# A graph layer with routed experts: tile 5 changes its group, the third group's slots go from 192 to 176, the last tile's steps stand one tick apart, and the third group's second biases are added by tile and share

## The chip, the cores and the metric

The kernel runs on one core of one Trainium2 chip. The metric is device time in microseconds (us) of one execution; less is better. The core has five engines that run beside each other and meet through semaphores: TensorE (PE: matmuls), VectorE (DVE), ScalarE (ACT), GpSimd (POOL, here it issues the gathers and scatters) and SyncE (SP, issues transfers). Loads of weights into the PE array are listed apart, as PEld.

## The reference, cut to what matters

There are 3125 nodes of 256 features and 100,000 edges, sorted by their target node (many more edges end at low nodes). The layer adds to the input an edge part (a maximum over the incoming edges of each node) and an attention-like part, and then a part in which a router picks two of eight experts for each node:

```python
xn = _layernorm(x)
x = x + gnn(xn, src, dst) + mix(xn)      # gnn: relu(theta(x_dst - x_src) + phi(x_src)),
                                         # maximum over the edges of each dst
# routed experts, on xt = layernorm(x)
probs = softmax(xt @ Wr + br)
top_p, top_idx = top_k(probs, 2)
weights = top_p / top_p.sum(-1)
xn = normalised(xt)
xe = xn * ln_g[e] + ln_b[e]              # for each expert e of 8
h  = gelu(xe @ W1[e] + b1[e])            # 256 -> 1024
y  = h @ W2[e] + b2[e]                   # 1024 -> 256
x  = x + sum of the two picked experts' y, times weights
```

All is computed in float32. `b2` is what is called the second bias.

## The kernel before, in words

**Tiles, groups, steps.** The nodes are 25 tiles of 128. The edges are walked from the highest target to the lowest. They are dealt out over 128 lanes (partitions), so one step handles 128 edges: one gather on POOL (line 107, `g<-b_d,srcI`) brings 128 rows of 256, and one fold on DVE (line 366) carries a running maximum along each lane. There are 755 such steps, in four groups. `GROUPS` says which tiles a group has, and `STEPS` how many steps its edges take: before, tiles 12 to 24 in 240 steps, tiles 6 to 11 in 161, tiles 1 to 5 in 228 and tile 0 in 126. Folded rows are stored to `s_d`, and a tile later fetches its nodes' rows from there with one gather each (`r<-s_d,end_i`).

**What follows a group.** When a group's last edge is folded, `carry` (lines 369 to 390) hands the maxima over from lane to lane: transposes on PE (L373), a scan on DVE (L378), transposes back (L384), a copy (L389). Then each tile of the group goes through `token_tile` (lines 422 to 495): selection matmuls (L445), a sum on DVE, moments, a scaling on ACT (`xt`, L471), transposes (L482), the router's matmul (L489, L491) and the top two (L494). For each half of the group's tiles `dispatch` works out weights (`shares`) and places (`slots`), and scatters the tiles' rows into the experts' lots in DRAM (`xs_d`, line 114). `CAPS` is the number of places an expert has in a group. The group then joins the queue of expert units (`Stream`): for each expert, eight steps f of `hp` (L615), gelu (L617) and, one unit later, `yp` (L639). A unit's `yp` matmuls are laid beside the next unit's `hp` matmuls; the last unit's close the stream alone. Before it is copied out, each `yp` gets the second bias of its expert from a matmul on 8 rows (L748). Results go to `ys_d` and are gathered again by `combine` (`g<-ys_d,from_i`), where L1299 weighs and adds them, and an `out` transfer on SP stores them.

**The last group.** Tile 0 alone is the fourth group. It isn't scattered: `dense_tile` runs all eight experts on its 128 rows and adds them with the router's weights (L822, L824). It starts when tile 0 is routed and the expert stream is through. Tile 0 needs two more things: the last six folded rows, picked by matmuls (L1278) with ones that `last_ends` prepares (lines 1245 to 1272), and the maxima of the first four nodes from edges beyond the 755 steps, which `first_maxima` (lines 1203 to 1240) works out on DVE from the whole of `b_d`, 100 operations in all. `dense_half` loads half of an expert's weights (1,024 KB) into a buffer that has come free. Combines wait for the flag `shared`, which stands for tile 0's weights being worked out; of the ten wide buffers' users at the end, several wait for an earlier user's `out` transfer.

**What sets the order.** PE, DVE, ACT and SP run in an order that a planner in the program writes out. Its unit is a tick, one gather issued on POOL (`TICK` stands for 1.25 us). Every piece of work is a generator that says by `yield n` after how many ticks its next step is to be placed. A queue of tasks with due times puts all pieces in one order, and a step placed later stands later in its engine's queue, ready or not. `on_pe` books time on PE, and the expert stream places its next step by it:

```python
def room(least=0.25):
    return max(least, clock["pe"] - clock["now"] - 2)
```

In `token_tile`, `at_once` shortens the distances between a tile's steps; before, to two ticks at most, for the third group and for tile 0.

Of the kernel before, what the change touches and what calls it, by code (L numbers as in the profile page):

```python
# [40 lines left out]
GROUPS = ((12, 25), (6, 12), (1, 6), (0, 1))  # L41
STEPS = (240, 161, 228, 126)
CAPS = (512, 256, 192)
LOT = (256, 256, 192)
# [23 lines left out]
def gps_layer(ctx: ExitStack, tc: tile.TileContext, x, src, dst, thetaT, phiT, gbias, wq, wkvT,  # L68
# [300 lines left out]
    def carry(pool, ps, g, last, chain, carried):  # L369
# [5 lines left out]
        yield 3  # L375
# [5 lines left out]
        yield 2  # L381
# [4 lines left out]
        yield 3  # L386
# [35 lines left out]
    def token_tile(work, ps, i, r1, slices, carried, top, top_i, newton=False, then=None,  # L422
                   also=None, at_once=False):
# [4 lines left out]
        def after(ticks):  # L428
            return min(ticks, 2) if at_once else ticks
# [67 lines left out]
    def shares(ro, i0, i1, top, top_i, made, wait=0):  # L497
# [9 lines left out]
        pick = ro.tile([P, 2, nt, E], F32, name="pick")  # L507
# [92 lines left out]
    class Units:  # L600
# [3 lines left out]
        def __init__(self, ps, act, whole=False):  # L604
            self.ps, self.act, self.behind, self.whole = ps, act, None, whole

        def run(self, e, w1t, xe, w2t, done, between, parts, part):
# [16 lines left out]
            self.behind = [hT, w2t, done, {}, parts, part]  # L624

        def second(self, f):
# [3 lines left out]
            hT, w2t, done, yp, per, part = self.behind  # L630
# [4 lines left out]
            for k in range(f * per, (f + 1) * per):  # L635
                r, q = k // FC, k % FC
                if q == 0:
                    yp[r] = self.ps.tile([P, D], F32, name="yp")
                nc.tensor.matmul(yp[r][0:part, :], hT[q][:, r * part:(r + 1) * part], w2t[:, q, :], start=(q == 0),  # L639
                                 stop=(q == FC - 1 and self.whole))  # L640
# [11 lines left out]
    class Stream:  # L652
# [29 lines left out]
        def rows(self, v):  # L682
            if 2 * v < len(self.lots) and ("xs", v) not in self.held:
                xs = self.held["xs", v] = self.at(v % 2)
                move(nc.scalar, self.as_two(xs, v), self.two(xs_d, v))
# [29 lines left out]
        def go(self):  # L715
# [5 lines left out]
            while True:  # L721
# [23 lines left out]
                def done(r, yp, u=u, ys=ys):  # L745
                    g, e, h = self.lots[u]
                    n = self.half(u)
                    nc.tensor.matmul(yp[0:n, :], ident[0:E, e:e + 1].to_broadcast([E, n]), b2_sb, start=False, stop=True)  # L748
# [17 lines left out]
                for _ in units.run(e, w1t, self.held["xe", u], w2t, done, between, 2, self.half(u)):  # L766
                    yield room()
# [13 lines left out]
    def dense_tile(act, ps, mm, i, shared, w, next_w, order=range(E), ready=None):  # L781
# [36 lines left out]
        units = Units(ps, act, True)  # L818
        for k, e in enumerate(order):
# [13 lines left out]
            for _ in units.run(e, w[e][0], held["xe", e], w[e][1], done, between, 1, P):  # L833
# [268 lines left out]

    def dispatch(g, half, i0, i1, top, top_i, taken):

        ro = at_hand["route"]
        while not all(i in routed for i in range(i0, i1)) or len(taken) < half:
# [4 lines left out]
        rest = shares(ro, i0, i1, top[:, at:at + i1 - i0, :], top_i[:, at:at + i1 - i0, :], made,  # L1111
                      15 if g == G - 2 and half == 0 else 0)
        start(rest, clock["now"] + next(rest))
        yield from slots(ro, mm, g, half, i0, i1, made[0], taken)
        yield 3 if g == G - 2 else 9
# [7 lines left out]
    def group(g):  # L1123
# [7 lines left out]
        start(carry(at_hand["tok"], mm, g, clock["last"], chain, carried), clock["now"] + (2 if g == G - 1 else 0))  # L1131
        yield STORED if g < G - 1 else 0
        if g == G - 1:
# [4 lines left out]
                              newton=True, then=lambda: start(dense), also=ends, at_once=True))  # L1138
# [413 lines left out]
```

## Time and profile before

| what | us |
|---|---|
| median of 3 runs | 1233.48 |
| the three runs | 1220.97, 1233.55, 1233.48 |
| the profiled execution's own time | 1227.71 |
| its span, first to last instruction | 1225.8 |
| PE busy in the span | 936.1 (76%) |
| POOL busy | 886.6 (72%) |
| DVE busy | 677.0 (55%) |
| ACT busy | 326.9 (27%) |
| mean granted PE clock | 0.857 |

The page's second part cuts the span into 40 slices of 30.6 us; a digit is the busy share of an engine in tenths. A row of its fifth part names line, engine, operation, result<-operands and count, then busy time and mean ns of one, then the idle time of the engine just ahead of it and what ended it. In a timeline the columns are start, duration, engine, line, operation and, in brackets, the idle time before and what released the instruction.

### The profile page before, as it was taken

The page shows a single profiled execution, that of the slowest core. Times are in us where ns is not written, and L with a number is a line of the kernel's source. Part 1 is how long each engine was busy: PE and PEld are TensorE (multiplying, and loading weights), DVE is VectorE, ACT ScalarE, POOL GpSimd, SP SyncE. Part 2 cuts the span into 40 slices and gives each one's busy share as a digit, 9 for nine tenths or more (in the row PEclk, how much of TensorE's full clock was granted, in tenths as well). Part 3 has the DMA queues.
Part 4 walks back from the last instruction along what each step waited for, and adds up shares of the span by engine and source line. Part 5 has one row for each costly group of instructions (what it writes and reads, how often), then busy time and mean ns, then how long its engine had stood idle before and what let it go on. Part 6 is the DMA issues. An engine that isn't in the chain of part 4 may idle for free.

```text
span 1225.8 us, 13367 instructions
## 1 busy us (share of the span) xinstructions
PE 936.1 (76%) x3931; PEld 671.4 (55%) x3931; DVE 677.0 (55%) x1989; ACT 326.9 (27%) x763; POOL 886.6 (72%) x911
## 2 busy tenths in 40 slices
PE   6547766736923449599999999999994619999895
PEld 4324333323301334268888788888883408786794
DVE  7669766675336682333338845564565843333533
ACT  4212222210101232043333333333330204332241
POOL 6677777777777777777767777777777777776433
PEclk9778988876965557889999999999996559999898
DMA  8668877666686763468887888999997559996583
GB/s 280 210 206 284 296 243 240 224 226 206 214 287 200 256 222 138 158 236 288 300 278 239 292 279 310 326 317 368 398 373 278 191 185 331 394 385 206 164 341 89
DMA packets 104268, 320.52 MB, mean 261 GB/s; under 512 B 20982, under 2 KB 44399, under 8 KB 92666
## 3 DMA queue, kind: packets, MB, share of 16 engines
q0 software_dynamic: 44032, 119.73, 30.8%
q1 hardware_dynamic: 29740, 115.08, 23.9%
q10 hardware_dynamic: 30414, 84.76, 19.5%
q8 instruction: 33, 0.54, 0.2%
q14 instruction: 49, 0.40, 0.1%
HBM read 192.18 MB, written 127.31 MB: 261 GB/s over the span
## 4 chain that ended last, share of the span: by engine, by line
PE 39%; DMA 23%; POOL 16%; issue 10%; DVE 10%; ACT 1%; ACTq 0%; POOLq 0%; DVEq 0%; SPq 0%
DMA g<-b_d,srcI 18%; POOL g L107 15%; PE yp L639 15%; PE hp L615 14%; DVE g L366 4%; DMA g<-ys_d,from_i 3%; PE yp L748 3%; PE bp L241 2%; PE mm L403 2%; DMA r<-s_d,end_i 1%; PE mm L401 1%; PE trf L693 1%; POOL xs_d L114 1%; PE tr L234 1%; PE am L445 0%
## 5 line engine op out<-in xcount | busy, mean ns | idle before, releaser
L107 POOL DMA_INDIRECT g<-b_d,srcI x755 | 739.4, 979 | 237.3 <-issue 203.2
L366 DVE SCALAR_TENSOR_TENSOR g<-g,cut 128x256 f32<-128x256 f32 x751 | 363.2, 484 | 345.3 <-DMA g<-b_d,srcI 326.5
L639 PE MATMUL yp<-w,hT 128*128 128x256 f32 (+1 forms) x1120 | 295.4, 386 | 5.3 <-DVE o L824 5.3
L615 PE MATMUL hp<-xe,w 128*128 128x256 f32 (+2 forms) x1216 | 285.2, 361 | 4.5 <-issue 1.7
L615 PEld LDWEIGHTS hp<-xe,w 128*128 128x128 f32 x1216 | 217.2, 195 | 39.8 <-issue 11.9
L617 ACT ACTIVATE hT<-hp,sm 128x256 f32<-128x256 f32 (+2 forms) x320 | 141.2, 441 | 326.2 <-PE hp L615 325.3
L639 PEld LDWEIGHTS yp<-w,hT 128*128 128x128 f32 (+1 forms) x1120 | 202.1, 186 | 44.3 <-issue 11.5
L1007 PE MATMUL kv<-wkv,xn_lo 128*128 128x512 f32 x96 | 52.8, 701 | 42.0 <-DVE kn L1025 28.2
L1007 PE MATMUL kv<-wkv,xn_hi 128*128 128x512 f32 x104 | 59.1, 722 | 31.1 <-DVE kn L1025 31.1
L107 POOL DMA_INDIRECT g<-ys_d,from_i x48 | 45.8, 955 | 42.5 <-DVE g L1299 14.8
L445 PE MATMUL am<-cr,oh 128*128 128x257 f32 x88 | 38.9, 574 | 33.6 <-DVE r L450 26.3
L1222 DVE SCALAR_TENSOR_TENSOR xn_lo<-xn_lo,no_edge 128x256 f32<-128x256 f32 x96 | 46.1, 480 | 28.5 <-DMA xn_lo<-b_d 28.5
L1007 PEld LDWEIGHTS kv<-wkv,xn_lo 128*128 128x128 f32 x96 | 20.7, 226 | 66.2 <-issue 63.2
L1007 PEld LDWEIGHTS kv<-wkv,xn_hi 128*128 128x128 f32 x104 | 22.9, 232 | 58.6 <-issue 54.5
L445 PEld LDWEIGHTS am<-cr,oh 128*128 128x128 f32 x88 | 21.7, 277 | 42.6 <-issue 32.7
L401 PE MATMUL mm<-bias,ones 1*128 1x512 f32 x50 | 31.8, 719 | 16.8 <-ACT x_sb L408 13.5
L748 PE MATMUL yp<-b_sb,ident 8*128 8x256 f32 (+1 forms) x128 | 43.9, 422 | 0.0
L1011 ACT ACTIVATE sq<-kv 128x1024 f32<-128x1024 f32 x25 | 25.5, 1019 | 52.7 <-PE kv L1007 52.7
L1019 ACT ACTIVATE rsk<-var,eps 128x16 f32<-128x16 f32 x25 | 7.7, 307 | 118.1 <-DVE var L1016 118.1
L704 ACT ACTIVATE xe<-trf,sm 128x256 f32<-128x256 f32 (+1 forms) x64 | 31.6, 547 | 24.0 <-PE trf L693 24.0
L1030 PEld LDWEIGHTS dots_p<-kn,vn 128*128 128x128 f32 x200 | 26.7, 197 | 19.1 <-issue 17.5
L1030 PE MATMUL dots_p<-kn,vn 128*128 128x128 f32 x200 | 27.6, 282 | 9.0 <-DVE kn L1025 9.0
(285 smaller groups left out, 978.3 us busy)
## 6 DMA issues: line engine op xcount, KB each, us to landing
s_d<-g SPq DMA_DIRECT2D x80, 1024.0 KB
w<-in_w ACTq DMA_DIRECT2D x84, 512.0 KB
w<-in_w ACTq DMA_DIRECT2D x6, 2048.0 KB
g<-b_d,srcI POOLq DMA_INDIRECT x755, 4.4
s_d<-g SPq DMA_DIRECT2D x13, 896.0 KB
xn_hi<-xs_d ACTq DMA_DIRECT2D x12, 512.0 KB
xs_d<-zero ACTq DMA_DIRECT2D x8, 512.0 KB
b_d<-bt SPq DMA_DIRECT2D x5, 640.0 KB
```

The lines of the kernel that those rows point to most:

```text
L107: got = nc.gpsimd.indirect_dma_start(out=to, out_offset=None, in_=table, in_offset=row_index(index))
L366: nc.vector.scalar_tensor_tensor(g[:, j, :], last, cut[:, t:t + 1], g[:, j, :], op0=OP.add, op1=OP.max)
L401: nc.tensor.matmul(am, ones[0:1, :], bias, start=True, stop=False)
L445: nc.tensor.matmul(r2, picks[k], carried[g], start=(k == 0), stop=(k == len(slices) - 1))
L615: nc.tensor.matmul(hp[:, 0:n], w1t[:, c, f, :], xe[:, c, 0:n], start=(c == 0), stop=(c == 1))
L617: nc.scalar.activation(hT[f][:, 0:n], hp[:, 0:n], AF.Gelu, bias=sm[:, 4 + f, e:e + 1])
L639: nc.tensor.matmul(yp[r][0:part, :], hT[q][:, r * part:(r + 1) * part], w2t[:, q, :], start=(q == 0), stop=(q == FC - 1 and self.whole))
L704: nc.scalar.activation(xe[:, c, 0:n], self.held["tr", u][:, c, 0:n], AF.Identity, bias=sm[:, 2 + c, e:e + 1], scale=sm[:, c, e:e + 1])
L748: nc.tensor.matmul(yp[0:n, :], ident[0:E, e:e + 1].to_broadcast([E, n]), b2_sb, start=False, stop=True)
L1007: nc.tensor.matmul(kv[:, k, :], xnT(i, c), wkv[:, c, k * INNER:(k + 1) * INNER], start=(c == 0), stop=(c == 1))
L1030: nc.tensor.matmul(dots_p[:, r, :], vn[:, r * P:(r + 1) * P], knf[:, r * P:(r + 1) * P], start=(i == 0 and r == 0), stop=(i == NT - 1), sk ...
L1222: nc.vector.scalar_tensor_tensor(of_k[:, k, :], b, no_edge[:, k, i:i + 1], of_k[:, k, :], op0=OP.add, op1=OP.max)
```

## The change

It has six parts.

- Tile 5 goes from the third group to the second, with the steps of its edges: `GROUPS` and `STEPS`. The sum of the steps stays 755.
- The third group's places for an expert go from 192 to 176.
- The third group's second biases are no longer added to each expert's `yp` by L748. A new function, `second_biases`, adds them to the tiles' rows in `x_sb`, from the two weights and the picked experts, with a transpose and one matmul for each tile. `Units` gets `whole` with each unit, so that the accumulation ends with the last `yp` matmul where no bias follows. The `pick` tile that it reads gets a buffer of its own for the half whose weights come late.
- The last group's `carry` steps and tile 0's `token_tile` steps stand one tick apart; `carry` is placed half a tick after the last fold and not two. The third group's scatter is placed one tick after its slots and not three.
- The first transfer of the third group's rows to the experts is two transfers, one for each of its two experts.
- `first_maxima` pauses while the third group's tiles are routed. The load of expert 0's first half and `last_ends` follow at its end; before, they followed 40 ticks after the third group had joined the queue.

```diff
-GROUPS = ((12, 25), (6, 12), (1, 6), (0, 1))
-STEPS = (240, 161, 228, 126)
-CAPS = (512, 256, 192)
-LOT = (256, 256, 192)
+GROUPS = ((12, 25), (5, 12), (1, 5), (0, 1))
+STEPS = (240, 195, 194, 126)
+CAPS = (512, 256, 176)
+LOT = (256, 256, 176)
...
 def carry(pool, ps, g, last, chain, carried):
...
-        yield 3
+        yield 3 if g < G - 1 else 1
...
-        yield 2
+        yield 2 if g < G - 1 else 1
...
-        yield 3
+        yield 3 if g < G - 1 else 1
...
 def token_tile(...):
-            return min(ticks, 2) if at_once else ticks
+            return min(ticks, at_once) if at_once else ticks
...
 def shares(...):
-        pick = ro.tile([P, 2, nt, E], F32, name="pick")
+        pick = ro.tile([P, 2, nt, E], F32, name=f"pick{int(wait > 0)}")
...
 class Units:
-                                 stop=(q == FC - 1 and self.whole))
+                                 stop=(q == FC - 1 and whole))
...
 class Stream, rows:
-                move(nc.scalar, self.as_two(xs, v), self.two(xs_d, v))
+                to, of = self.as_two(xs, v), self.two(xs_d, v)
+                if self.lots[2 * v][0] == G - 2 and self.lots[2 * v][1] == 0:
+                    for k in range(2):
+                        move(nc.scalar, to[:, k], of[:, k])
+                else:
+                    move(nc.scalar, to, of)
...
 done:
-                    nc.tensor.matmul(yp[0:n, :], ident[0:E, e:e + 1].to_broadcast([E, n]), b2_sb, start=False, stop=True)
+                    if g < G - 2:
+                        nc.tensor.matmul(yp[0:n, :], ident[0:E, e:e + 1].to_broadcast([E, n]), b2_sb, start=False,
+                                         stop=True)
...
+    def second_biases(i0, i1, pick):
+        ro = at_hand["route"]
+        for t in range(i1 - i0):
+            i = i0 + t
+            by = ro.tile([P, 2, E], F32, name="by2")
+            for k in range(2):
+                nc.vector.tensor_scalar(by[:, k, :], pick[:, k, t, :], share[:, k, i:i + 1], None, op0=OP.mult)
+            nc.vector.tensor_add(by[:, 0, :], by[:, 0, :], by[:, 1, :])
+            yield 1
+            bt_p = mm.tile([E, P], F32, name="mm")
+            nc.tensor.transpose(bt_p, by[:, 0, :], ident)
+            on_pe(0.3)
+            yield 3
+            bt = ro.tile([E, P], F32, name="bt2")
+            nc.vector.tensor_copy(bt, bt_p)
+            yield 2
+            bb = mm.tile([P, D], F32, name="mm")
+            nc.tensor.matmul(bb, bt, b2_sb, start=True, stop=True)
+            on_pe(0.5)
+            yield 3
+            nc.vector.tensor_add(x_sb[:, i, :], x_sb[:, i, :], bb)
...
 dispatch:
+        def rest():
+            yield from shares(...)
+            if g == G - 2:
+                yield from second_biases(i0, i1, made[0])
...
-        yield 3 if g == G - 2 else 9
+        yield 1 if g == G - 2 else 9
...
 group:
+        if g == G - 2:
+            clock["tokens"] = True
-        start(carry(...), clock["now"] + (2 if g == G - 1 else 0))
+        start(carry(...), clock["now"] + (0.5 if g == G - 1 else 0))
...
-                              newton=True, then=lambda: start(dense), also=ends, at_once=True))
+                              newton=True, then=lambda: start(dense), also=ends, at_once=1))
...
         if g == G - 2:
+            clock["routed"] = True
             start(verdict())
-            yield 40
-
-            dense_half(0, 0, xn_lo[:, 1:1 + FC, :].rearrange("p i d -> p (i d)"))
-            yield from last_ends()
...
 first_maxima:
+            while "tokens" in clock and "routed" not in clock:
+                yield 1
...
+        dense_half(0, 0, xn_lo[:, 1:1 + FC, :].rearrange("p i d -> p (i d)"))
+        yield from last_ends()
```

## The prediction, made blind

> **What bounds the kernel now.** I read the page first, then POOL's timeline from end to end, then PE's and DVE's timelines from 1000 us. Of the page two rows matter: POOL is never dense, never empty, up to slice 36, and PE has a hole in slices 30 to 32.
>
> ```profile
> PE   6547766736923449599999999999994619999895
> ...
> POOL 6677777777777777777767777777777777776433
> ...
> L107 POOL DMA_INDIRECT g<-b_d,srcI x755 | 739.4, 979 | 237.3 <-issue 203.2
> ```
>
> The 755 gathers have 0.30 us of issue time before each, and in POOL's list of waits from 84 to 1115 us the only long one is 2.6 us on a store. So POOL issues without a pause, one gather in about 1.25 us, up to 1115.2. The changed kernel issues the same number before that point (755 edge gathers, 24 row gathers, 48 scatters; they are only dealt out differently). That stretch is therefore fixed, and everything to be won lies after it. PE's timeline there:
>
> ```profile
> 1010.67 0.90 PE L693 MATMUL trf<-ident,xn_hi 96*128 96x96 f32 x4 [19.27 <-DMA xn_hi<-xs_d]
> ...
> 1114.32 2.47 PE L1278 MATMUL am<-g,xn_lo 128*128 128x256 f32 x8
> ...
> 1119.56 0.70 PE L1278 MATMUL am<-g,xn_lo 128*128 128x256 f32 x2 [1.64 <-DVE g L366]
> ...
> 1123.25 0.64 PE L373 MATMUL mm<-ident,g 128*128 128x128 f32 x2
> ...
> 1133.45 0.38 PE L384 MATMUL mm<-ident,ct 128*128 128x128 f32 x2
> ...
> 1134.53 0.60 PE L445 MATMUL am<-cr,oh 128*128 128x257 f32 x2
> ...
> 1139.28 0.67 PE L748 MATMUL yp<-b_sb,ident 8*96 8x256 f32 x2
> ...
> 1143.93 2.08 PE L615 MATMUL hp<-xe,w 128*128 128x128 f32 x8 [0.90 <-DVE xe L797]
> ...
> 1211.78 6.28 PE L639 MATMUL yp<-w,hT 128*128 128x256 f32 x16 [5.32 <-DVE o L824]
> ```
>
> The third group's expert units run from 1010.67. PE reaches the six picks (L1278) at 1114.32, waits for the last fold until 1120.26, and only then does the rest of the units. In between stand tile 0's steps; L384 starts at 1133.45, though its operand ct was ready at 1125.0. The dense tile starts at 1143.93, and its last 16 matmuls wait 5.3 us for DVE's L824, which stands behind the combines (L1299). Those are late for another reason, which POOL's timeline shows:
>
> ```profile
> 1119.27 1.06 POOL L107 DMA_INDIRECT r<-s_d,end_i  x1 [4.05 <-issue]
> ...
> 1162.20 0.94 POOL L107 DMA_INDIRECT g<-ys_d,from_i  x1 [11.73 <-DMA out<-g]
> ...
> 1191.37 0.94 POOL L107 DMA_INDIRECT g<-ys_d,from_i  x1 [14.47 <-DVE g L1299]
> ```
>
> After the last edge POOL waits 4 us with tile 0's row gather for the last store. The gathers of ys_d then stop twice for a wide buffer. At 1162.20 it is freed by the first out transfer (issued 1158.55, 2.9 us); before 1191.37 the third out transfer, issued at 1174.08, shares the DMA engines with three 2,048 KB weight loads.
>
> **What the Trainium skill says.** "TensorE: Matmul & The Clock Gate", section The mechanism: "MATMULs are pc-monotone in start AND end", strict FIFO. The trace agrees (L384 above). So the planner's order on PE, not the data alone, decides when tile 0 gets on. "DMA: Bandwidth & Descriptors", section Issuing engines are not separate DMA queues: transfers from SP, ACT and POOL interleave on the same 16 engines; the trace agrees (an out transfer of 512 KB in 2.9 us at 1158.55, about 16 us at 1174.08). The same page, section Anatomy of one DMA, gives about 2.0 us fixed plus bytes over 436 GB/s; used once below.
>
> **The change, part by part.** A tick is one gather, 1.25 us.
>
> *Groups and steps.* Tile 5 moves to the second group, whose edges end 34 steps later (435, not 401): 42.5 us. Its row gathers start at 630.7 + 42.5 = 673.2, the seventh 6 x 8.8 us later at 726; the last scatter ended 55 us after the last row gather (675.2 to 730.4), now at about 783, and the group joins the unit queue at about 790. PE reaches the end of the first group's units at 792 (units every 15.9 us, the last of 24 begins at 903.6). It would find nothing fetched: rows, transposes and scaling take 12 ticks, so the 17th unit starts at about 804. But the closing half of the 16th, otherwise laid beside it, has then been done, and the units end some 5 us after 927.7. The third group's routing begins on PE at 939.7: covered. If that cover were gone, routing would queue behind units at 1.7 us a step. Second-group scatters had slot_i ready at 720.6 for an issue at 722.1: with a seventh tile POOL may stand there; bounds 0 and 4 us, since row gather to top took 32 to 36 us for all six tiles without growing; I take 1.
>
> *Third group's start.* Four tiles: the last row gather is the fourth (961.71), later by the three POOL issues moved ahead of it (3.8 us), so 965.5 for 966.97. The scatter was due 26 ticks later, now 24 (the yield of 3 made 1): 995.5, not 1000.16. slot_i was ready at 993.3, a slack of 6.9 us; cutting 2.5 stalls nothing. xs in two halves lets the first transposes go about 0.45 us sooner (half of 384 KB by the skill's formula, an estimate); behind it PE idles, so the end gains nothing.
>
> *176 slots.* In the steady stream four records of L615 take 0.65 us net at 192 columns and 0.866 at 256, so they go by width: 0.596 at 176, and 64 steps save 3.5 us. L639 keeps its 256 columns. The reference's own router puts at most 147 rows of tiles 1 to 4 and 243 of tiles 5 to 11 on one expert, so neither 176 nor 256 overflows, and the general path is not entered.
>
> *Second biases.* 32 records of L748, 10.7 us busy, about 9.6 net, leave PE. In their place come four transposes (0.27) and four pairs on 8 rows (0.69): 4 us, and 4 x 5 short DVE operations (0.2 to 0.45). The planner puts them at ticks 35 to 53 after the second row gather and 20 to 38 after the fourth, all before the first unit (some 46 after the fourth), where PE idles (19.3 us before L693). Without that cover: 4 us plus eight crossings of up to 1.6 (L815's wait).
>
> *first_maxima.* Held while the third group's tiles run, it gives DVE 0.48 us a step back there; its last four tiles and the transposes (1.6 us on PE) fall into the units. It, the 1,024 KB load and last_ends are through by about 1076; needed at 1115.
>
> *What the units win.* By ticks, starting 3.7 earlier, 56 steps at 1.161 for 1.204 (2.4; the planner books 0.43 us per 128 columns of L615 and 0.86 of L639), less 2.3 for the transposes inside: some 4 ticks, 3 or 4 steps more before the picks. PE had f0 to f3 of the last expert done; now f0 to f6. Behind the picks stay one step (1.46) and eight closing ones (0.87): 8.4 us, where 17.1 stood. The other 9 us are not won as time: PE waits for the last fold at 1119.5 anyway.
>
> *Tile 0.* L373 comes directly after the picks, L384 two ticks later, the last L445 two after that, where it took five and three. 1120.3 + L373 0.64 + one step 1.46 + six L445 2.03 + L384 0.38 = 1124.8; copy and crossing 0.6; two closing steps beside it end at 1126.5; L445 0.60: 1127.1. The row r is folded in at 1124.3, earlier. From there 6.1 us to xt (1135.16 to 1141.27) and 2.7 to the dense tile (to 1143.93): 1135.9, with the 1 us of POOL 1136.9. That is 7.0 us earlier. The six closing steps left (5.2) fit into the 6.1.
>
> *Dense tile and combines.* 62.5 us to 1206.4, less the 1.7 us stop at 1197.4 for an xe behind combines: done at 1197.7. Tile 0's router steps now precede the dense matmuls, so shares are there about 1140 (for 1151.5). The first out transfer then frees its buffer near 1148, before POOL asks (1151); the two 1,024 KB loads are over before the three of 2,048 KB begin at 1156.8, and 7.8 MB at some 390 GB/s end near 1177, not 1190. Fourteen gathers (17.5) plus 3.1 landing: L824 free at 1198.2, PE waits about 1 instead of 5.3. 1198.7 + 6.3 + the 7.7 us that follow L824 in the profile = 1212.7, so **-13.1 us**.
>
> The profiled execution took 1227.71 (span 1225.8); the sum gives 1214.6. The runs' median stands 5.8 above it, so I carry the difference over: **1220.4**.
>
> **The rivals.** *Rigid tail:* the combines stay bound to the weight loads, which move with the dense start; 5.3 and 1.7 remain. -7.0: 1226.5. For it: L824's wait and the 16 us transfer. Against: the two 1,024 KB loads move further. *More:* fewer steps stand between tile 0's, r alone ends last (1124.3 + 6.1 + 2.7 = 1133.1, -10.8), and L815's 1.6, the 1.7 and the 5.3 all go: -19.4, 1214.1. *Slower:* on PE's queue, what remains of the units is ordered behind tile 0's closely set L482 and L489; some 9.5 us fit ahead of them (three steps up to L445, then one each 0.7 tick for five ticks), every further one holds the dense tile from 1136.9 on, so it turns to a loss above 16.5. If the third group starts late because the second group's units still fill PE during its routing, and 22 us remain, the dense tile starts at 1149.5: +5.6, 1239.1. Against: 12 us between 927.7 and 939.7. Overflow is ruled out above.
>
> **How the numbers follow.** Forecast 0.48, rigid 0.24, more 0.14, slower 0.14. About 1% (12.3 us) is what a measurement of this kernel can tell from no change; its three runs already span 1220.97 to 1233.55. Faster by over 1%: 0.38 of the forecast, 0.13 of more, 0.03 of rigid, 0.54. Slower by over 1%: 0.08, if more than 22 us remain. Within: 0.38. The range runs from just under "more" less half a per cent (1208) up to 1236, most of the way to the slower case.
>
> **What would show it.** Right: L693 for the third group under 1010, no L748 after it, nine or ten steps of L639 after the picks, dense L615 near 1136, no 14 us stop of POOL, under 2 us before the last L639. Wrong: POOL stops at the scatters near 770, units of the third group still running at 1140, or the 5 us wait for L824 unchanged.

## The result, and the profile after

| what | before | after |
|---|---|---|
| median of 17 runs each, us | 1230.88 | 1224.6 |
| lowest run, us | 1220.97 | 1214.11 |
| profiled execution, us | 1227.71 | 1217.18 |
| its span, us | 1225.8 | 1215.1 |

The ratio of the runs is 0.9948 with a 95% interval of 0.9926 to 0.997, so the change saves 0.5% (3.7 to 9.1 us of 1230.9). The prediction said 1220.4 with a range of 1208 to 1236. The time is in the range, but the gain is half of the 13.1 us that was forecast, and it is in the class "within 1%", to which 0.38 was given, not in the likelier class "faster". As a gain it is nearer to the 7.0 us of the rival "rigid tail" than to the forecast. One run of 17 took 1864.67, and seven of the runs below fell on chips where the kernel before, too, took about 1780; such numbers are not compared with the others.

The two rows of the page that the prediction started from, now of the kernel after:

```profile
PE   6557766745942548779999999979999527999896
...
POOL 6677777777777777777777777777777777776743
```

PE's hole between the second group's units and the third's, digits 4, 6, 1 before, is 5, 2, 7 now and lies one slice later, since the second group's units end later. POOL is as even as before. The table of the stretches shows the third group's units (1010 to 1115) and the first part of the tail, first of the kernel before, then of the kernel after. Columns: window, length, busy time and count of PE, PEld, DVE, ACT, POOL, then clock, DMA share and GB/s.

```profile
1010.00:1115.00 105.00, 101.71 (x519) 82.47 (x519) 40.57 (x92) 37.35 (x89) 80.02 (x83) 0.97 0.97 361
1145.00:1165.00 20.00, 18.37 (x106) 16.72 (x106) 10.80 (x35) 7.07 (x20) 6.44 (x8) 0.82 0.51 168
```

```profile
1010.00:1115.00 105.00, 95.91 (x499) 80.92 (x500) 44.50 (x106) 35.16 (x88) 80.42 (x81) 0.90 0.99 361
1145.00:1165.00 20.00, 19.97 (x134) 17.81 (x135) 9.89 (x25) 8.56 (x24) 9.52 (x10) 1.00 0.99 363
```

Two things are to be seen. PE lost 5.8 us of work in the units' stretch (part of it because the units now start 2 us later), and the stretch moved the same 361 GB/s with the DMA engines full. From 1145 to 1165 the DMA engines were half idle before (0.51); after, they are full (0.99). The combines' transfers and the weight loads now use time that nobody used.

PE's timeline of the kernel after, from the third group's start to the end:

```profile
1006.56 1.22 PE L1128 MATMUL mm<-b_sb,bt 8*128 8x256 f32 x2 [5.34 <-DVE odd_f L1215]
1011.30 0.37 PE L1121 MATMUL mm<-ident,by 128*8 128x128 f32 x1 [3.52 <-DVE by L1118]
...
1012.75 0.85 PE L698 MATMUL trf<-ident,xn_hi 88*128 88x88 f32 x4
...
1125.41 0.70 PE L1318 MATMUL am<-g,xn_lo 128*128 128x256 f32 x2 [1.94 <-DVE g L366]
...
1138.22 0.44 PE L482 MATMUL mm<-ident,xt 128*128 128x128 f32 x2 [2.55 <-ACT xt L471]
...
1140.45 2.80 PE L639 MATMUL yp<-w,hT 128*88 128x256 f32 x12
1143.09 1.05 PE L615 MATMUL hp<-xe,w 128*128 128x128 f32 x8
...
1187.14 0.68 PE L615 MATMUL hp<-xe,w 128*128 128x128 f32 x4 [2.40 <-issue]
...
1203.36 4.05 PE L639 MATMUL yp<-w,hT 128*128 128x256 f32 x18
```

The first unit (L698) stands in order behind the second biases (L1121, L1128), which wait for DVE (below). The picks end later than before (1125.41, not 1119.56). Twelve closing matmuls stand behind tile 0's router and hold the dense tile until 1143.09. Then there is one stop of 2.40 us for an xe, and none before the last L639, where 5.32 us stood. POOL's stops behind the last edge (1118.26):

```profile
1169.11 0.95 POOL L107 DMA_INDIRECT g<-ys_d,from_i  x1 [10.63 <-DVE g L1339]
...
1180.90 0.95 POOL L107 DMA_INDIRECT g<-ys_d,from_i  x1 [2.08 <-DMA out<-g]
```

With a stop of 1.52 at 1156.26 these are 14.2 us of stops among the gathers of ys_d, where 29.1 (11.73, 14.47 and two of 1.39 and 1.51) stood. The row of 10.63 names DVE's L1339, but POOL waits there for an out transfer too: the one issued at 1156.08, whose last part is recorded at 1168.35, just as POOL's wait ends. The same goes for the 1.52: that wait ends with the transfer of 1147.04, which is through at 1155.50. So these two out transfers take 8.5 and 12.3 us beside weight loads, where the two that POOL waited for before took 2.9 and 16.5.

### The profile page after: what moved, and what is told of

Read it like the earlier page. It is cut to its first block, busy times and chain, and to the rows that moved or that the text cites. A ratio compares the mean times of both kernels' runs of the same rounds, so it can differ in the third digit from the quotient of the medians.

```text
span 1215.1 us, 13342 instructions
## 1 busy us (share of the span) xinstructions
PE 940.2 (77%) x3909; PEld 673.2 (55%) x3909; DVE 682.5 (56%) x2018; ACT 325.4 (27%) x762; POOL 890.1 (73%) x911
## 4 chain that ended last, share of the span: by engine, by line
PE 33%; DMA 26%; POOL 18%; issue 11%; DVE 10%; ACT 1%; ACTq 0%; SPq 0%; POOLq 0%; DVEq 0%
DMA g<-b_d,srcI 20%; POOL g L107 17%; PE hp L615 11%; PE yp L639 11%; DVE g L366 4%; DMA xn_lo<-b_d 3%; PE bp L241 2%; PE mm L403 2%; PE yp L754 1%; DMA r<-s_d,end_i 1%; PE mm L401 1%; DMA ys_d<-ys 1%; POOL xs_d L114 1%; PE am L445 1%; PE tr L234 1%
## 5 line engine op out<-in xcount | busy, mean ns | idle before, releaser
L639 PE MATMUL yp<-w,hT 128*128 128x256 f32 (+1 forms) x1120 | 296.6, 387 | 0.0
L615 PE MATMUL hp<-xe,w 128*128 128x256 f32 (+2 forms) x1216 | 286.7, 361 | 10.7 <-DMA w<-in_w 4.3
L615 PEld LDWEIGHTS hp<-xe,w 128*128 128x128 f32 x1216 | 218.1, 197 | 46.8 <-issue 13.5
L639 PEld LDWEIGHTS yp<-w,hT 128*128 128x128 f32 (+1 forms) x1120 | 202.0, 185 | 36.9 <-issue 9.4
L107 POOL DMA_INDIRECT g<-ys_d,from_i x48 | 46.7, 974 | 27.9 <-issue 13.1
L445 PE MATMUL am<-cr,oh 128*128 128x257 f32 x86 | 37.6, 563 | 26.6 <-DVE r L450 19.8
L1014 PEld LDWEIGHTS kv<-wkv,xn_hi 128*128 128x128 f32 x104 | 23.6, 239 | 55.7 <-issue 51.8
L445 PEld LDWEIGHTS am<-cr,oh 128*128 128x128 f32 x86 | 20.8, 272 | 35.8 <-issue 24.8
L107 POOL DMA_INDIRECT keys<-in_dst,run_i x25 | 23.8, 954 | 13.2 <-issue 7.3
```

Of the source, the lines that this page charges most:

```text
L107: got = nc.gpsimd.indirect_dma_start(out=to, out_offset=None, in_=table, in_offset=row_index(index))
L445: nc.tensor.matmul(r2, picks[k], carried[g], start=(k == 0), stop=(k == len(slices) - 1))
L615: nc.tensor.matmul(hp[:, 0:n], w1t[:, c, f, :], xe[:, c, 0:n], start=(c == 0), stop=(c == 1))
L1014: nc.tensor.matmul(kv[:, k, :], xnT(i, c), wkv[:, c, k * INNER:(k + 1) * INNER], start=(c == 0), stop=(c == 1))
```

## The experiments

Three theories were set against each other. **A**: the gain comes from the close steps of carry and tile 0, which bring the router's weights (`full`) earlier and so free the combines. **B**: it comes from the lighter third group, which leaves less behind the picks. **C**: the move of the second biases wins nothing, since the units' PE work is hidden under weight loads and under the wait for the last fold. The new groups, the 176 places, the earlier scatter, the split transfer and the pause of `first_maxima` have no comparable run of their own; where "the rest of the change" is said below, it is these together.

The table puts all profiles that can be compared side by side. The ratio is that of the runs, with its 95% interval; the other columns are starts, differences of two starts, or sums of stops, each in that kernel's own profile. "Fold" is the last fold on DVE, "dense" the first L615 on the dense tile, "full" the step that completes tile 0's weights (L786, before L779), "last o" the last sum L831 (L824 before), and "stops" POOL's stops of over 0.4 us between the gathers of ys_d.

| kernel | ratio to before | last edge at | fold at | fold to dense | fold to full | stops | dense to last o |
|---|---|---|---|---|---|---|---|
| before | | 1114.27 | 1119.02 | 24.9 | 32.4 | 29.1 | 74.2 |
| after | 0.9948 (0.9926 to 0.997) | 1118.26 | 1124.87 | 18.2 | 18.3 | 14.2 | 64.4 |
| after, old distances | 0.9986 (0.9968 to 1.0003) | 1115.19 | 1119.92 | 18.6 | 26.1 | 21.7 | 71.1 |
| before, close steps | 0.996 (0.994 to 0.998) | 1116.73 | 1121.60 | 21.7 | 18.8 | 15.7 | 66.6 |
| after, biases back | 0.9932 (0.9912 to 0.9953) | 1117.49 | 1123.33 | 16.5 | 18.4 | 14.1 | 66.6 |
| after, xe on ACT | 0.9973 (0.9952 to 0.9993) | 1118.74 | 1122.82 | 23.6 | 18.6 | 21.6 | 66.8 |
| biases back, later xe on ACT | 0.9928 (0.9905 to 0.9952) | 1128.00 | 1133.61 | 16.5 | 18.4 | 9.2 | 59.4 |

The fold and the step `full` on DVE, before and then after:

```profile
1119.02 0.48 DVE L366 SCALAR_TENSOR_TENSOR g<-g,cut 128x256 f32<-128x256 f32 x1 [1.86 <-DMA g<-b_d,srcI]
...
1151.42 0.17 DVE L779 TENSOR_TENSOR full<-by 128x8 f32<-128x8 f32 x1
```

```profile
1124.87 0.48 DVE L366 SCALAR_TENSOR_TENSOR g<-g,cut 128x256 f32<-128x256 f32 x1 [2.35 <-DMA g<-b_d,srcI]
...
1143.15 0.17 DVE L786 TENSOR_TENSOR full<-by 128x8 f32<-128x8 f32 x1
```

**The close steps taken out of the kernel after.**

```diff
 def carry(...):
-        yield 3 if g < G - 1 else 1
+        yield 3
...
-        yield 2 if g < G - 1 else 1
+        yield 2
...
-        yield 3 if g < G - 1 else 1
+        yield 3
...
-        start(carry(...), clock["now"] + (0.5 if g == G - 1 else 0))
+        start(carry(...), clock["now"] + (2 if g == G - 1 else 0))
...
-                              newton=True, then=lambda: start(dense), also=ends, at_once=1))
+                              newton=True, then=lambda: start(dense), also=ends, at_once=2))
```

> The changed kernel with the last group's carry and tile 0's steps at their old distances, on a chip whose kernel before takes about 1230. In PE's order all closing steps of the units then stand ahead of L482, and L489 and L491 stand behind the first two dense hp. Theory A (the gain comes from the close steps): shares about 5 us later than the 1143.2 of the changed kernel, PE waits for L831 again, 5 to 8 us over the changed kernel, 1.000 to 1.003 of before. Theory B (the gain comes from the lighter third group): within 2 us of the changed kernel, 0.994 to 0.997.

Measured: 0.9986, some 4.7 us over the kernel after, just under the range that theory A gave and outside that of theory B; the interval reaches the edges of both. The place was not where A's expectation had it. PE and POOL of this kernel:

```profile
1138.50 2.08 PE L615 MATMUL hp<-xe,w 128*128 128x128 f32 x8 [0.90 <-DVE xe L804]
...
1141.03 1.02 PE L491 MATMUL mm<-wr_sb,xtT 128*128 128x8 f32 x4
```

```profile
1156.76 0.94 POOL L107 DMA_INDIRECT g<-ys_d,from_i  x1 [5.20 <-DMA out<-g]
...
1185.80 0.94 POOL L107 DMA_INDIRECT g<-ys_d,from_i  x1 [16.53 <-DMA out<-g]
```

The dense tile starts 18.6 us behind the last fold, as early as with the close steps (18.2). The close steps do not bring it forward. What they bring forward is `full`: 26.1 without them, 18.3 with them, since L489 and L491 stand behind dense matmuls here. The first out transfer is then issued at 1153.12 (33.2 us behind the fold, where the kernel after has 22.2) and the third at 1170.31, between the weight loads of 1167.03 and 1174.19. POOL stops 16.5 us for a buffer, and the dense tile takes 71.1 us and not 64.4. The wait for L831 is only 0.84. The time is in a stop of 2.17 for a bias that stands on DVE behind combines, in L489 and L491, which now stand inside the dense tile, and in PE's clock: the first eight records of L615 take 2.08 us and not 1.05 (see "Dense to last o" below). The stop of 2.39 for an xe has its like in the kernel after (2.40).

**The close steps alone, in the kernel before.** The same five lines, in the other direction.

> The kernel before with nothing but the close steps, on a chip whose kernel before takes about 1230. Theory A: the last edge stays at 1114, shares at about 1136, dense start about 1140, under 1 us of wait for L824: 0.990 to 0.994, as much as the whole change or more. Theory B: 0.998 to 1.003. Slower rival: the remainder behind L491 holds the dense tile beyond 1144, over 1.000.

Measured: 0.996, between what A and B expected: 4.9 us, where the whole change wins 6.4 (the intervals overlap). The slower rival's mechanism is seen at work:

```profile
1135.30 0.61 PE L491 MATMUL mm<-wr_sb,xtT 128*128 128x8 f32 x4
1135.77 2.81 PE L639 MATMUL yp<-w,hT 128*96 128x256 f32 x12
1138.51 0.67 PE L748 MATMUL yp<-b_sb,ident 8*96 8x256 f32 x2
1139.11 3.69 PE L639 MATMUL yp<-w,hT 128*96 128x256 f32 x16
1142.73 0.67 PE L748 MATMUL yp<-b_sb,ident 8*96 8x256 f32 x2
1143.33 1.16 PE L615 MATMUL hp<-xe,w 128*128 128x128 f32 x8
```

Tile 0's router is through at 1135.9, and 7.4 us of closing work stand between it and the dense tile, which starts 21.7 us behind the fold instead of 18.2. The early `full` (18.8) still takes the stops from 29.1 to 15.7 and the dense tile from 74.2 to 66.6. So the two parts do different things: the rest of the change, with its smaller remainder behind the picks, brings the dense tile forward (24.9 to 18.6 without close steps), the close steps bring the weights forward.

The runs say which of the two is worth more. The close steps win 4.9 us alone, and 4.7 are lost when they are taken out. The rest of the change wins 1.7 us alone (0.9986) and 1.5 on top of the close steps, neither clear of nothing. The parts add up, and the larger one is theory A's: an early dense tile by itself wins little here.

**The second biases back in the units.**

```diff
-                    if g < G - 2:
+                    if True:
                         nc.tensor.matmul(yp[0:n, :], ident[0:E, e:e + 1].to_broadcast([E, n]), b2_sb, ...
...
-                for _ in units.run(e, ..., between, 2, self.half(u), g == G - 2):
+                for _ in units.run(e, ..., between, 2, self.half(u), False):
...
-            if g == G - 2:
-                yield from second_biases(i0, i1, made[0])
```

> The changed kernel with the second biases in the third group's units again (L754 there, no second_biases). As the prediction booked it, 9.6 us net more on PE: the dense tile 5 to 8 us later, 0.999 to 1.002 of before. Theory C (the units' PE work is hidden under weight loads and under the wait for the last fold, and the first unit no longer waits behind L1121 and L1128): within 2 us of the changed kernel, 0.993 to 0.997.

Measured: 0.9932, not slower than the kernel after (0.9948; the intervals overlap). Theory C's numbers hold, and the 0.999 to 1.002 of the prediction's booking lies outside the interval.

```profile
1009.18 0.85 PE L698 MATMUL trf<-ident,xn_hi 88*128 88x88 f32 x4 [17.15 <-DMA xn_hi<-xs_d]
...
1123.87 0.70 PE L1316 MATMUL am<-g,xn_lo 128*128 128x256 f32 x2 [0.19 <-DVE g L366]
...
1139.24 0.66 PE L754 MATMUL yp<-b_sb,ident 8*88 8x256 f32 x2
1139.83 1.16 PE L615 MATMUL hp<-xe,w 128*128 128x128 f32 x8
```

With no bias in PE's order, the first unit waits for its rows alone and starts 108.3 us ahead of the last edge, where the kernel after has 105.5. PE comes to the last pick just as the last fold ends (a wait of 0.19). Of the 32 matmuls of L754, 26 stand ahead of the last pick. They are paid in time that PE would have waited: between the first L698 and the last pick PE is idle for 5.8 us, where the kernel after has 9.7, and that stretch begins 3.6 us earlier. The dense tile starts 16.5 us behind the fold.

**The dense tile's xe on ACT.** The 2.40 us stop was for an xe on DVE, ordered behind combines.

```diff
-                    nc.vector.tensor_scalar(held["xe", e][:, c, 0:P], xT[:, c, :], sm[:, c, e:e + 1],
-                                            sm[:, 2 + c, e:e + 1], op0=OP.mult, op1=OP.add)
+                    nc.scalar.activation(held["xe", e][:, c, 0:P], xT[:, c, :], AF.Identity,
+                                         bias=sm[:, 2 + c, e:e + 1], scale=sm[:, c, e:e + 1])
```

> The changed kernel with the dense tile's xe scaled on ACT (an activation with scale and bias, as the expert stream does) instead of on DVE, where it stands in order behind the combines' L1339. Theory A: what the tail still loses is order on DVE; the PE stop of 2.40 us at 1184.7 and the matmuls at half pace for some 4 us after it (about 2 us lost) go, so 3 to 4 us under the changed kernel, 0.991 to 0.993 of before. Rival (the last gather of ys_d at 1197.55 and the sums behind it set the end, not PE): PE then waits for DVE's L831 instead, and the run is within 1 us of the changed kernel, 0.994 to 0.996.

Measured: 0.9973, so neither: some 3 us over the kernel after, though the intervals overlap and this one reaches the rival's range. ACT and PE of the profile:

```profile
1144.67 0.37 ACT L756 COPY xn_hi<-yp 88x256 f32<-88x256 f32 x1 [3.99 <-PE yp L639]
...
1145.86 0.88 ACT L804 ACTIVATE xe<-xT,sm 128x128 f32<-128x128 f32 x2 [0.82 <-DMA ys_d<-xn_hi]
```

```profile
1146.41 1.91 PE L615 MATMUL hp<-xe,w 128*128 128x128 f32 x9 [1.77 <-ACT xe L804]
...
1200.46 1.22 PE L639 MATMUL yp<-w,hT 128*128 128x256 f32 x2 [4.36 <-DVE o L831]
```

The first xe now stands on ACT behind the last closing copy and two issues of transfers, and PE waits 1.77 us for it. That is a third of the 5.4 us by which the dense tile starts later behind the fold (23.6); the rest is not this edit's order on ACT: PE comes to the picks 1.6 us later behind the fold, and the last twelve closing matmuls take 4.88 us and not 2.80, most of that at half the clock (0.50 from 1137.2 to 1144.0). The stop for an xe is gone, but 4.36 us for L831 came in its place, as the rival had it: POOL stops 13.43 us for an out transfer again.

**Biases back, and on ACT only from the second expert on.**

```diff
+                    if k:
+                        nc.scalar.activation(held["xe", e][:, c, 0:P], xT[:, c, :], AF.Identity, ...)
+                    else:
                         nc.vector.tensor_scalar(held["xe", e][:, c, 0:P], ...)
```

> The second biases back in the third group's units, and the dense tile's xe from its second expert on scaled on ACT (the first stays on DVE, since on ACT it stood behind the closing copies and began the dense tile 3.3 us late). If PE's stop for xe (4.55 us with the biases back) is what is left to win: 3 to 5 us less than with the biases back alone, 0.988 to 0.991 of before. If the sums of the combines on DVE set the end behind it: PE waits for L831 instead, 0.992 to 0.995.

Measured: 0.9928, the value of the biases back alone (0.9932), so within the second expectation. Its profile says otherwise: PE has no stop of 1 us behind the picks, and the dense tile takes 59.4 us, 7.2 less than with the biases back alone. That profile owes its late last edge (1128.00) to stops of POOL long before anything that this edit touches, the longest one at the first group's scatters:

```profile
509.77 1.01 POOL L114 DMA_INDIRECT xs_d<-xn_hi,slot_i  x1 [6.97 <-issue]
```

The stops account for some 8.6 of its 13.7 us over the kernel before, longer gathers and scatters for the other 5.1. All that follows is shifted with it. That the runs do not show the 7.2 us as a gain means that one profile's tail is no measure of the kernel's; what the other executions lose stays open. No version beats the kernel after by more than the intervals can tell.

**The second group's scatters three ticks later**, on top of the last one:

```diff
-        yield 1 if g == G - 2 else 9
+        yield (9, 12, 1)[g]
```

> As the run before it (second biases back in the units, xe on ACT from the second expert on), with the second group's scatters placed 12 ticks after their slots and not 9. In the profiles of the new groups POOL stands 1.2 to 3.0 us at the first of these scatters (near 750) and 0.8 to 2.4 us at the second (near 777), for slot_i. If POOL's stream up to the last edge sets the end, as the prediction has it: these two stops go, the last edge comes 2.5 to 3.8 us sooner, 0.990 to 0.991 of before. Rival (the second group joins the unit queue 4 us later, its units end later and hold the third group's routing, or the tail is set by weight loads that do not move with the last edge): 0.992 to 0.995.

Measured: 0.997 (0.9914 to 1.0025), where the kernel before took 1778.52. Inconclusive: POOL stopped for some 480 us ahead of the last edge, and the two scatters waited 24.6 and 26.4 us among them.

**Runs where the kernel before took about 1780.** The first three of these kernels ran there as well. The old distances in the kernel after came out at 0.9984 (0.9946 to 1.0021) and 0.9893 (0.9853 to 0.9933), against

> The changed kernel with the last group's carry and tile 0's steps at their old distances. Theory A (the gain of the change comes from tile 0's closely set steps: earlier shares, so that the combines' buffers come free in time): shares about 5 us later than in the changed kernel (1148 for 1143.2), the 5 us wait for L831 (old L824) comes back, and the run is 5 to 8 us over the changed kernel, 1.000 to 1.003 of the kernel before. Theory B (the gain comes from the lighter third group: fewer slots, no biases in its units, less left over behind the picks): within 2 us of the changed kernel, 0.994 to 0.997 of before.

> The changed kernel with the last group's carry and tile 0's steps at their old distances, on a chip whose kernel before takes about 1231. Theory A (the gain comes from the close steps): shares about 5 us later than in the changed kernel, the wait ahead of the last L639 comes back, 5 to 8 us over the changed kernel, 1.000 to 1.003 of the kernel before. Theory B (the gain comes from the lighter third group): within 2 us of the changed kernel, 0.994 to 0.997.

The close steps alone came out at 0.9925 (0.9852 to 0.9998) and 1.0005 (0.9952 to 1.0058), against

> The kernel before with nothing but the close steps of the last group's carry and of tile 0. In PE's order seven closing steps and two second biases then stand behind L491, 6.8 us. Theory A: shares at about 1136 instead of 1151.5, dense start about 1140 instead of 1143.9, the 5.3 us wait for L824 gone: 8 to 10 us less than before, 0.992 to 0.994, as much as the whole change. Theory B: without the smaller remainder behind the picks the close steps win nothing, since the closing steps now stand between L491 and the dense tile: 0.998 to 1.003. Slower rival of the prediction: the remainder holds the dense tile beyond 1144, over 1.000.

> The kernel before with nothing but the close steps, on a chip whose kernel before takes about 1231. Theory A: shares at about 1136, dense start about 1140, no wait for L824: 0.992 to 0.994, as much as the whole change or more. Theory B: 0.998 to 1.003. Slower rival: seven closing steps behind L491 hold the dense tile beyond 1144, over 1.000.

The biases back came out at 0.9858 (0.9813 to 0.9903), against

> The changed kernel with the second biases added in the third group's units again (L754 there, no second_biases). As the prediction booked it: 32 matmuls, 9.6 us net more on PE between 1010 and 1140, PE reaches the picks after the last fold and the dense tile starts 5 to 8 us later, 0.999 to 1.002 of before. Theory C (the units wait for weight loads, DMA share 1.0 from 1050 to 1115, so PE work in them is hidden, and the first unit no longer waits behind L1121 and L1128): first trf near 1007 instead of 1012.75, end within 2 us of the changed kernel, 0.993 to 0.997.

The same kernel twice differs by 0.9% in the first case, more than its intervals allow, and by 0.8% in the second, so none of the theories is judged by these runs. On the chips of the table only the kernel before was measured more than once, so a difference of this kind between the rows can't be excluded either. A further one had the groups, steps and 192 slots of before, with the biases back:

```diff
-GROUPS = ((12, 25), (5, 12), (1, 5), (0, 1))
-STEPS = (240, 195, 194, 126)
-CAPS = (512, 256, 176)
-LOT = (256, 256, 176)
+GROUPS = ((12, 25), (6, 12), (1, 6), (0, 1))
+STEPS = (240, 161, 228, 126)
+CAPS = (512, 256, 192)
+LOT = (256, 256, 192)
```

> The changed kernel with the groups, steps and 192 slots of before and with the second biases back in the units; kept are the close steps, the scatter one tick after its slots, the split transfer and the pause of first_maxima. In PE's order one step and eight closing steps stand behind the picks, as in the changed kernel. Theory C (the new groups and the biases ahead of the first unit cost what the tail wins): last fold back near 1119.5, dense start about 1138, 4 to 6 us less than the changed kernel, 0.989 to 0.992 of before. Theory B: the lighter third group is missing, so within 2 us of before, 0.998 to 1.002.

Measured: 1.0058 (1.0024 to 1.0092), but this kernel does not compute the layer: its output is off by a relative 0.25, and why is open. Nothing is built on it, so the worth of the new groups by themselves was not settled.

## Why the prediction was right, point by point

The forecast's mechanism was a tail that is shorter because the dense tile starts earlier and the combines' buffers come free earlier. The profile shows the first, and of the second a half: one of POOL's two long stops went, the other stayed at 10.63 us of 14.47. Its sum was -13.1 in the profile; the profiles differ by -10.5, the medians by -6.3. The terms of the profile:

| term | forecast | measured |
|---|---|---|
| last fold | +1 | +5.85 |
| fold to dense | -8.0 | -6.7 |
| dense to last o | -6.1 | -9.8 |
| span | -13.1 | -10.7 |

That the sum comes near is luck in part: the last fold was 4.85 us later than forecast and the dense tile 3.7 us shorter, and the two misses mostly cancel. In the runs the gain is that of "rigid tail" (7.0), though its mechanism, stops that stay as they were, is not what the profile shows.

**POOL's stream, "That stretch is therefore fixed".** This is the step that failed. The last edge came 4.0 us later, and its rows and fold took another 1.85 (6.6 us from issue to fold, not 4.75). The bound of 4 us held the first, the value of 1 did not. POOL did stand at the second group's scatters in the kernel after:

```profile
749.04 1.18 POOL L114 DMA_INDIRECT xs_d<-xn_lo,slot_i  x1 [1.77 <-ACT hT L617]
...
776.57 1.00 POOL L114 DMA_INDIRECT xs_d<-xn_lo,slot_i  x1 [0.77 <-ACT hT L617]
```

(ACT is a bystander: slot_i itself was written by DVE at 748.1.) All five comparable profiles of the new groups have 2.5 to 3.8 us there. But the old groups with close steps have more:

```profile
697.72 1.18 POOL L114 DMA_INDIRECT xs_d<-xn_lo,slot_i  x1 [3.61 <-ACT xe L704]
```

Summed over all stops above 0.36 us between the first edge and the last, each less the usual 0.30, the seven profiles of the table have, in its order, 3.2, 4.5, 7.7, 6.7, 6.9, 5.2 and 11.8 us. The profile before was the one with the fewest. But the stops are only 1.3 of the 4.0 us. POOL's 826 gathers and scatters in that stretch were themselves busy for 813.8 us, where the kernel before had 811.1 for as many, and the seven profiles lie between 807.8 and 816.2. The stream is no constant but a minimum, to which each execution adds stops and longer gathers: the last edge lay between 1114.27 and 1118.74 in six of seven. How much of the 4.0 us is the new groups' and how much chance stays open.

**Second group's units.** They ended at 941.5, 13.8 us later than 927.7; about 5 was said. The cover held: routing's first step on PE came at 945.2 instead of 939.7.

**Third group's start, "L693 under 1010".** Wrong: L698, as it is called now, stands at 1012.75. The scatters came about as forecast (the second one at 997.95; 995.5 was said). But "all before the first unit, where PE idles" overlooked what the biases themselves wait for. On DVE:

```profile
1005.96 0.48 DVE L366 SCALAR_TENSOR_TENSOR g<-g,cut 128x256 f32<-128x256 f32 x1 [4.38 <-DMA g<-b_d,srcI]
1006.36 0.15 DVE L1215 TENSOR_REDUCE odd_f<-mm 1x1 f32<-1x7 f32 x1
```

A fold waits 4.38 us for its gather, and the short operations behind it that PE's L1128 needs wait with it (5.34 us on PE). The 1.6 us a crossing that was named as the price without cover was too small. In the end it cost nothing that the runs show: with the biases back they are as fast. What the split transfer wins can't be read here, since the rows did not set the start; its 0.45 us came from a figure that the Trainium skill, "DMA: Bandwidth & Descriptors", section Anatomy of one DMA, gives for transfers issued by GpSimd, and these are issued by ACT.

**Units.** Right: one step and eight closing ones stand behind the picks. That PE still waited for the last fold was luck. It had done the other picks by 1123.47; with the last fold where the forecast had it, over by 1120.5, PE would have been some 3 us late for it.

**Tile 0 and the dense start.** The last L445 came 6.6 us behind the start of the last fold, where 8.1 was said (1127.1 - 1119.0), and L482 at 13.3, where 14.2 was said. But behind that L445 eight closing steps were left, not six, and they did not "fit into the 6.1": the planner put four of them ahead of L482, one between, and three behind L491, where 2.65 us of them stand ahead of the dense tile. This is the slower rival in small. In the kernel before with close steps alone it is 7.4 us.

**What brings the dense tile forward.** The prediction's sum won the 7.0 us by closer steps on a smaller remainder. The run without close steps starts as early behind the fold (18.6), so in this kernel the rest of the change does it; that the remainder is what counts in that rest is argued from PE's order, and no run changes it alone. In the kernel before, the close steps bring the dense tile forward too (24.9 to 21.7). In the kernel after they act through `full`, which comes at 1143.2 where the forecast had 1140.

**Combines.** Right in part: no wait before the last L639, and the DMA engines took the combines and loads in 1145 to 1165. The first out transfer was issued at 1147.04 but ended at 1155.50, not "near 1148": it ran in the stretch whose DMA engines are now full (0.99), beside two loads of 1,024 KB. It cost POOL 1.52 us. The stop of 10.63 us was not foreseen. It is of the same kind as the 14.47 before it: the second out transfer took 12.3 us beside the weight loads. Here "rigid tail", which bound the combines to the weight loads, was right in kind, but the 5.3 us that it kept are gone; "more" needed an order on PE that didn't come. "1.7 stop gone" was wrong: 2.40 stands there.

**Dense to last o, -9.8 for -6.1.** The sum priced waits on PE at their length and left PE's clock out. The 5.32 us wait cost more than itself: the 16 matmuls behind it took 6.28 us, where the 18 of the kernel after take 4.05. The dense tile also began slowly before: its first eight L615 took 2.08 us and the next 28 took 5.78, where the kernel after has 1.05 and 4.22. By an estimate from these rows that is 2.7 and 2.6 us. Another 1.4 are L489 and L491, which stood inside the dense tile before and stand ahead of it now. Against it, the 2.40 us stop was not in the sum, and matmuls behind it are slow as well: four records of L615 take 1.06 us and not 0.61.

The Trainium skill, "TensorE: Matmul & The Clock Gate", section What's actually happening, says that the array's clock is halved after an idle window of some 3.4 us. The trace agrees on the window, but it need not be idle throughout. In the seven profiles of the table the granted clock is either 1.00 or 0.50, it changes on a fixed grid of 3.41 us, and whether a stretch at 1.00 is followed by one at 0.50 goes with how long PE was busy in it. In the kernel after, 1.47 us of work in 1122.90 to 1126.31 and 1.00 in 1184.34 to 1187.74 were each followed by a stretch at 0.50. The longer stop of 2.55 us ahead of L482 was not: the grid cuts it, and PE was busy for 2.52 and 1.73 us in its two stretches. In the kernel before, 1.47 us of work in 1138.47 to 1141.88 came just ahead of the dense tile, and the clock stayed at 0.50 up to 1152.1. From 1016 us on, every stretch at 1.00 with less than 1.4 us of work was followed by one at 0.50, none with more than 2.2 was, and between them both happened. So it matters where a stop falls on the grid, along with its length.

**From the profile to the runs.** 5.8 us were carried over from the profile to the median of three runs. Over 17 runs the median before lies 3.2 us above its profile, the median after 7.4 above its own. Of the 6.8 us by which the medians miss the -13.1, the three terms above account for 2.4; the rest is between this profile and its kernel's median, and no run shows what it is.

## What to carry to other kernels

Split a tail into what starts it and what feeds it. Here less left-over work started the dense tile earlier, and that alone won too little to be told from nothing; earlier router weights, which let the combines go, won most of the time. Before work is moved off an engine, ask whether the stretch it leaves is bound by that engine; 32 matmuls left PE where transfers and the last fold set the pace, and the operations that replaced them held the first unit in PE's order. A stream that looks fixed in one profile should be given the spread that other profiles show, and a wait on PE the slow matmuls that can follow it. A releaser that a view names for a wait on several semaphores is a suggestion: the 10.63 us stop here was an out transfer's, not DVE's.

## What the runs showed of the hardware

On the chips where the kernel before took about 1780 us, engines got each other's signals late. In the profile of the kernel before, all 778 of PE's signals are recorded within 0.2 us of the end of the instruction that gave them. In one of the runs there (the kernel after with the old distances, in its second set), 173 of 770 have no signal on record until more than 2 us after it; only 665 signals are on record at all, so some of these may be missing and not late. One of ACT's gelus in another, with the biases back, which PE releases:

```profile
718.59 0.47 ACT L617 ACTIVATE hT<-hp,sm 128x256 f32<-128x256 f32 x1 [10.75 <-remote]
```

PE's matmuls for it had ended at about 710, and its signal is recorded at 718.57. POOL's gathers ran at their usual 0.95 us in the same profile. Here the signal was late and not missing, since ACT starts with it. What delays the signals no run shows. The kernel before takes 45% longer there; whether the late signals are all of it is not shown either, and the mean granted clock of the profiles is lower there too (0.74 for 0.85). A comparison of fractions of a per cent needs the time of the kernel before on the same chip first.
